# All additions of a Haar mixing phase on GpSimd, its transfers as single DMAs over 128 partitions, and the next phase's first work placed in the last rounds of the one before

## The chip, the cores and the metric

The kernel runs on one core of a Trainium2 chip. The metric is device time in microseconds (us), the median of several runs. Each profile is of one execution.

Short names used below: PE is TensorE, DVE is VectorE, ACT is ScalarE, POOL is GpSimd, SP is the engine that issues the DMAs.

## The reference

Four layers act in turn on x, a float32 array of shape (4, 64, 256, 256): a long convolution, a Haar layer with channel mixing, and two more long convolutions.

```python
def long_conv(x, ...):                      # layers 0, 2, 3
    k = outer product of two implicit filters per channel
    y = irfft2(rfft2(x, 512x512) * rfft2(k) / 512**2)[..., :256, :256]
    return y + x * bias[:, None, None]

def haar_layer(x, v, conv_w, tau):          # layer 1; v, tau (2,1,1,256,256), conv_w (2,64,64)
    f1 = haar2d(x)
    acc = 0
    for i in range(2):
        f4 = einsum('bchw,oc->bohw', f1 * v[i], conv_w[i])
        acc = acc + sign(f4) * relu(abs(f4) - tau[i])
    return haar2d(acc, inverse=True) + x
```

The kernel does each long convolution as two multiplications by Toeplitz matrices, one along each axis, because the filter is an outer product. Since the Haar transform is linear, `+ x` becomes an addition of the coefficients f1 to acc.

## The kernel before

There are three phases. **A** does layer 0 and the forward transform, channel pair by channel pair, and stores coefficients. **B** mixes the channels: a partition holds one channel of one half of the image rows, so 128 partitions are 64 channels by 2 halves. **C** does the inverse transform and layers 2 and 3. The four images are split into two groups. B's first half (group 0) runs beside A's second group, and B's second half (group 1) beside C's first group. "Beside" is literal: each phase is a list of small pieces, and the pieces of two lists are issued alternately.

```python
# phase A, one piece: rows, then columns, then products of the round before (each a third of a round)
def piece(t, j):
    now, last = t < total, t > 0
    ...
    if j < M:
        if now:  rows(t, j)                   # matmuls, eviction on ACT
        if last: run(st[t - 1]["ops"], 2)     # sums of the Haar transform, GpSimd
    elif j < 2 * M:
        if now:  columns(t, j - M)            # matmuls, then x1 = x*bias + psum on DVE (L302)
        ...
    else:
        if last: product(t - 1, j - 2 * M)    # matmuls with the Haar matrix
        if now:  run(st[t]["ops"], 2)
for t in range(total + 1):                    # the last turn has only products
    ...

# phase B, group grp; a unit u is one of the two mixings of a step of two image rows
def load(s):
    d["f"], d["v"], d["tau"] = ...            # 128-partition tiles, 4, 3 and 3 buffers
    for g in range(2):                        # two halves of 64 partitions
        part = slice(g * C, (g + 1) * C)
        nc.sync.dma_start(d["f"][part]..., coef[grp][:, rows]...)
        nc.sync.dma_start(d["v"][part]..., flat(v[rows]))
        nc.sync.dma_start(d["tau"][part]..., flat(taus[rows]))

def mix(u):                                   # PSUM pool of two buffers
    un[u]["f4"] = bps.tile([P, 2, W], F32, tag="f4", ...)
    for j in range(2):
        nc.tensor.matmul(un[u]["f4"][:, j, :], mix_sb[:, u % 2, :], f[:, j, :], ...)
def multiply(u):   nc.vector.tensor_tensor(f4, f4, v, ALU.mult)
def sign(u):       nc.scalar.activation(m, f4, AF.Sign)
def magnitude(u):  nc.scalar.activation(f4, f4, AF.Abs)
def less(u):       nc.vector.tensor_tensor(f4, f4, tau, ALU.subtract)
def threshold(u):
    o = un[u]["f4"] if u % 4 == 3 else un[u]["m"]
    nc.vector.scalar_tensor_tensor(o, un[u]["f4"], 0.0, un[u]["m"], ALU.max, ALU.mult)
def add(s, which):
    if which == 0:  nc.gpsimd.tensor_tensor(m0, m0, data(st[s]["f"]), ALU.add)
    elif s % 2:     nc.vector.tensor_tensor(g, m0, un[2 * s + 1]["f4"], ALU.add)   # L438
    else:           nc.gpsimd.tensor_tensor(g, m0, un[2 * s + 1]["m"], ALU.add)

def piece(u, j):
    s, i = divmod(u, 2)
    if j == 0:    mix(u); less(u - 1)
    elif j == 1:
        multiply(u); sign(u)
        threshold(u - 1); add((u - 1) // 2, 1 - i)
        if i == 0 and s >= 2:
            store(s - 2); load(s + 2)         # the store too: two halves of 64 partitions
    else:         magnitude(u)
...
# phase C, at its first piece
if t == 0:
    load(0); load(1); sums(0); run(st[0]["ops"], 16); filters(0)
...
beside(a[cut_a:], phase_b(0), 5 * M, M)
beside(c[:cut_c], phase_b(1), 2 * M, 10 * M)
beside(c[cut_c:], [], 0, 0)
```

In these traces each engine runs its instructions in the order in which the kernel issues them; a timeline further down shows VectorE idle for 1.14 us before A's L302, with B's multiply behind it in the order of issue, although the matmul that the multiply needs had ended. Two things follow. The next mix needs one of the two PSUM buffers, so it waits for the threshold (or, every fourth time, the addition) of the unit before last. And A's column addition L302 is on DVE in the same order as B's multiply.

## Time and profile before

| | before |
|---|---|
| device time | 3161.6 us (3160.7 to 3162.8, 3 runs) |
| PE busy | 2973.0 us of a span of 3159.3 us (94%) |
| A with B (first to last mix of B's first half) | 774 us, 6.10 us a mix, PE idle 94 us |
| handover (last mix to the first mix of B's second half) | 55 us, PE idle 31 us |
| C with B (B's second half) | 940 us, PE idle 13 us |
| DMA share in A with B | 1.03 at 269 GB/s |

The unit of 6.10 us is 774.1 us over the 127 distances between 128 mixes. The DMA share is the packets' time, summed, over the time of 16 engines; at 1, packets of all 16 DMA engines are in flight all the time, and it goes a little over 1 where packets overlap.

To read the page: the rows of 40 digits are slices of 79 us, a 9 being busy nine tenths or more. In a row of the costliest groups the numbers are the total busy time and the mean of one instruction, then the idle time of that engine just before those instructions, and what ended most of it. The POOL row of the page of the kernel before, and its row for the mixing matmul:

```profile
POOL 2776675666766766655556555565664444444441
...
L409 PE MATMUL f<-ft,mix_sb 128*128 128x512 f32 x1024 | 506.1, 617 | 112.6 <-DVE gt L438 57.3
```

GpSimd has room everywhere (no slice reaches 80%), and the mixing matmul is the only one of PE's with a large idle time before it. Its own mean of 617 ns will matter too.

### The profile page before, as it was taken

How to read it: one execution, taken by the hardware profiler on the slowest of the kernel's cores; microseconds unless marked ns; L12 is line 12 of the kernel's file. 1: busy time of each engine (PE TensorE's matmuls, PEld its weight loads, DVE VectorE, ACT ScalarE, POOL GpSimd, SP SyncE). 2: the span in 40 equal slices, each digit the busy share in tenths (PEclk: the TensorE clock that was granted, in tenths of full speed). 3: DMA queues.
4: the chain of work that ended last, by engine and by line, in shares of the span. 5: the costliest groups of instructions: out<-in, count | busy, mean ns of one | idle time of the engine just before them, and what ended most of it. 6: DMA issues, size and time to landing. Idle time of an engine off the chain costs nothing. (4 is left out here: it accounts for less than half of the span.)

```text
span 3159.3 us, 48195 instructions
## 1 busy us (share of the span) xinstructions
PE 2973.0 (94%) x17432; PEld 2535.1 (80%) x17432; DVE 1564.9 (50%) x1657; ACT 1230.2 (39%) x1799; POOL 1817.4 (58%) x2437
## 2 busy tenths in 40 slices
PE   5999999888988888599999999999999999999999
PEld 5989997666666666488877878887899999999998
DVE  2232213777777777457666667666732222222222
ACT  1333333444544445344444444444432222232222
POOL 2776675666766766655556555565664444444441
PEclk9999999999999999899999999999999999999999
DMA  6857898999999999789888988989744444444442
GB/s 159 215 179 193 226 234 226 258 274 272 274 275 270 274 277 265 230 195 268 233 244 226 250 231 238 249 226 255 205 141 132 141 124 124 124 138 132 127 120 87
DMA packets 380227, 656.76 MB, mean 208 GB/s; under 512 B 42134, under 2 KB 281399, under 8 KB 379992
## 3 DMA queue, kind: packets, MB, share of 16 engines
q1 hardware_dynamic: 379992, 653.69, 76.6%
q8 instruction: 140, 2.29, 0.3%
q14 instruction: 95, 0.78, 0.1%
HBM read 438.10 MB, written 215.42 MB: 207 GB/s over the span
## 5 line engine op out<-in xcount | busy, mean ns | idle before, releaser
L409 PE MATMUL f<-ft,mix_sb 128*128 128x512 f32 x1024 | 506.1, 617 | 112.6 <-DVE gt L438 57.3
L434 POOL TENSOR_TENSOR m<-m,ft 128x1024 f32<-128x1024 f32 x128 | 301.7, 2357 | 453.1 <-DVE m L429 441.4
L417 ACT ACTIVATE m<-f 128x1024 f32<-128x1024 f32 x256 | 262.5, 1025 | 513.1 <-DVE f L413 504.3
L546 DVE SCALAR_TENSOR_TENSOR cy<-cz,bias_sb,c1c 128x512 f32<-128x512 f32 x256 | 189.2, 746 | 515.9 <-PE c1c L224 515.9
L424 DVE TENSOR_TENSOR f<-f,tau 128x1024 f32<-128x1024 f32 x256 | 314.6, 1229 | 197.0 <-ACT f L420 194.2
L302 DVE SCALAR_TENSOR_TENSOR x<-x,bias_sb,a2ps 128x512 f32<-128x512 f32 x256 | 189.0, 745 | 428.8 <-PE a2ps L224 380.4
L409 PEld LDWEIGHTS f<-ft,mix_sb 128*128 128x128 f32 x1024 | 177.5, 193 | 258.3 <-issue 142.6
L546 DVE SCALAR_TENSOR_TENSOR o<-cy,bias_sb,c2c 128x512 f32<-128x512 f32 x256 | 189.5, 746 | 348.7 <-PE c2c L224 348.7
L413 DVE TENSOR_TENSOR f<-f,v 128x1024 f32<-128x1024 f32 x256 | 313.8, 1226 | 54.9 <-PE f L409 51.8
L223 PE MATMUL a1ps<-toep,x 128*128 128x256 f32 x1024 | 310.1, 385 | 21.3 <-DMA toep<-filt 18.1
L223 PE MATMUL a2ps<-toep,ay 128*128 128x256 f32 x1024 | 305.9, 381 | 1.8 <-ACT ay L292 1.8
L223 PE MATMUL c2r<-toep,cy 128*128 128x256 f32 x1024 | 305.8, 380 | 0.3 <-DVE cy L546 0.3
L223 PE MATMUL c1c<-toep,ch 128*128 128x256 f32 x1024 | 305.8, 380 | 0.0
L223 PE MATMUL c1r<-toep,cz 128*128 128x256 f32 x1024 | 305.8, 380 | 0.0
L223 PE MATMUL c2c<-toep,ch 128*128 128x256 f32 x1024 | 305.8, 380 | 0.0
L533 ACT COPY ch<-c2r 128x512 f32<-128x512 f32 x256 | 149.4, 588 | 382.4 <-PE c2r L224 382.2
L325 ACT ACTIVATE f<-a3ps,wcol_sb 128x512 f32<-128x512 f32 x256 | 175.7, 686 | 293.2 <-PE a3ps L317 251.5
L317 PEld LDWEIGHTS a3ps<-haarH_sb,fw 128*128 128x128 f32 x2048 | 244.9, 195 | 32.5 <-issue 22.7
L526 ACT COPY cz<-c1ps 128x512 f32<-128x512 f32 x256 | 148.1, 588 | 309.5 <-PE c1ps L522 309.5
L522 PEld LDWEIGHTS c1ps<-haarW_sb,ci 128*128 128x128 f32 x2048 | 238.8, 193 | 36.6 <-POOL ci L266 24.4
L522 PE MATMUL c1ps<-haarW_sb,ci 128*128 128x128 f32 x2048 | 244.6, 276 | 23.4 <-POOL ci L266 23.3
L420 ACT ACTIVATE f<-f 128x1024 f32<-128x1024 f32 x256 | 263.9, 1031 | 0.0
(64 smaller groups left out, 5868.5 us busy)
## 6 DMA issues: line engine op xcount, KB each, us to landing
toep<-filt SPq DMA_DIRECT2D x768, 128.0 KB, 4.1
x<-in_x SPq DMA_DIRECT2D x256, 256.0 KB, 7.8
coef<-f SPq DMA_DIRECT2D x128, 512.0 KB, 7.3
ft<-coef SPq DMA_DIRECT2D x256, 256.0 KB, 6.6
v<-in_v SPq DMA_DIRECT2D x256, 256.0 KB, 7.0
tau<-taus SPq DMA_DIRECT2D x256, 256.0 KB, 7.0
mixed<-gt SPq DMA_DIRECT2D x256, 256.0 KB, 6.0
g<-mixed SPq DMA_DIRECT2D x128, 512.0 KB, 5.4
```

The lines of the kernel that those rows point to most:

```text
L223: nc.tensor.matmul(ps[:, m, :], data[:, 0, cut], t[:, which, :], start=True, stop=False)
L302: nc.vector.scalar_tensor_tensor(s["x1"][:, cut], s["x"][:, cut], bias_sb[:, c : c + 1], ps, ALU.mult, ALU.add)
L317: nc.tensor.matmul(ps[:, e, bass.ts(k, P)], s["fw"][:, 2 * (n + e) + k, bass.ts(m, P)], haarH_sb[:, k, :], start=True, stop=True,)
L325: nc.scalar.activation(f4[:, n : n + 2, m, :], ps, AF.Copy, scale=wcol_sb[:, m : m + 1])
L409: nc.tensor.matmul(un[u]["f4"][:, j, :], mix_sb[:, u % 2, :], f[:, j, :], start=True, stop=True)
L413: nc.vector.tensor_tensor(f4, f4, weights(st[u // 2]["v"], u % 2), ALU.mult)
L417: nc.scalar.activation(un[u]["m"], un[u]["f4"], AF.Sign)
L420: nc.scalar.activation(un[u]["f4"], un[u]["f4"], AF.Abs)
L424: nc.vector.tensor_tensor(f4, f4, weights(st[u // 2]["tau"], u % 2), ALU.subtract)
L434: nc.gpsimd.tensor_tensor(m0, m0, data(st[s]["f"]), ALU.add)
L522: nc.tensor.matmul(ps[:, m, bass.ts(h, P)], s["ci"][:, 2 * n + h, bass.ts(m, P)], haarW_sb, start=True, stop=True)
L546: nc.vector.scalar_tensor_tensor(o, s["y", n], bias_sb[:, at : at + 1], ps, ALU.mult, ALU.add)
```

## The change

Three independent parts, which I name by a letter.

- **G**: every second step's addition moves from VectorE to GpSimd, which then does all of them. The point is to free the PSUM buffer one VectorE instruction earlier.
- **D**: partitions of B change their order from (half, channel) to (channel, half), so that each load and store of B is a single DMA over 128 partitions instead of two over 64.
- **P**: A's last turn (only products) is taken out of its list and put between C's first pieces. C's first loads and sums are issued in A's last two rounds, and B's first half is packed in front of those rounds.

The diff, cut to its core:

```diff
 # G
         def threshold(u):
-            o = un[u]["f4"] if u % 4 == 3 else un[u]["m"]
-            nc.vector.scalar_tensor_tensor(o, un[u]["f4"], 0.0, un[u]["m"], ALU.max, ALU.mult)
+            nc.vector.scalar_tensor_tensor(un[u]["m"], un[u]["f4"], 0.0, un[u]["m"], ALU.max, ALU.mult)
 ...
-                if s % 2:
-                    nc.vector.tensor_tensor(data(st[s]["g"]), m0, un[2 * s + 1]["f4"], ALU.add)
-                else:
-                    nc.gpsimd.tensor_tensor(data(st[s]["g"]), m0, un[2 * s + 1]["m"], ALU.add)
+                nc.gpsimd.tensor_tensor(data(st[s]["g"]), m0, un[2 * s + 1]["m"], ALU.add)
 # D   (mix_sb is built on the host in the new order; the first store's sums use a column of signs)
-            for g in range(2):
-                part = slice(g * C, (g + 1) * C)
-                rows = slice(g * C + r0, g * C + r0 + ROWS)
-                nc.sync.dma_start(d["f"][part]..., coef[grp][:, rows]...)
-                nc.sync.dma_start(d["v"][part]..., flat(v[rows]))
-                nc.sync.dma_start(d["tau"][part]..., flat(taus[rows]))
+            nc.sync.dma_start(d["f"].rearrange("p r b w -> p (r b w)"), rows_of(coef[grp], r0))
+            for name, src in (("v", v), ("tau", taus)):
+                flat = bass.AP(src.tensor, src.offset + r0 * 2 * W, [[0, C], [C * 2 * W, 2], [1, ROWS * 2 * W]])
+                nc.sync.dma_start(d[name].rearrange("p r i w -> p (r i w)"), flat)
+        def rows_of(ap, r0):
+            return ap.rearrange("c (g r) b h k -> c g r (b h k)", g=2)[:, :, r0 : r0 + ROWS].rearrange(
+                "c g r e -> c g (r e)")
 ...
-            for g in range(2):      # store, two halves
-                ...
+            nc.sync.dma_start(rows_of(mixed[grp], r0), gt.rearrange("p r b w -> p (r b w)"))
 # P
-        for t in range(total + 1):
+        for t in range(total):
 ...
+        last = [lambda: (coarsest(t - 1), store(t - 1), run(st[t]["ops"], 16))]
+        last += [lambda j=j: product(t, j) for j in range(M)]
+        last.append(lambda: (coarsest(t), store(t)))
 ...
-    beside(a[cut_a:], phase_b(0), 5 * M, M)
-    beside(c[:cut_c], phase_b(1), 2 * M, 10 * M)
+    beside(a[cut_a : -6 * M], phase_b(0), 5 * M, 0)
+    beside(a[-6 * M : -2 * M], c_first[:1], 2 * M, M)
+    beside(a[-2 * M :], c_first[1:], 0, 0)
+    main = a_last[:1] + c[:M]
+    for pair in zip(c[M : 2 * M], a_last[1:]):
+        main += pair
+    main += a_last[M + 1 :] + c[2 * M : cut_c]
+    beside(main, phase_b(1), 5 * M, 10 * M)
```

## The prediction

> **What bounds the kernel now.** I read the page first, for who is busy and when.
>
> ```profile
> PE 2973.0 (94%) x17432; PEld 2535.1 (80%) x17432; DVE 1564.9 (50%) x1657; ACT 1230.2 (39%) x1799; POOL 1817.4 (58%) x2437
> ...
> PE   5999999888988888599999999999999999999999
> ...
> PEclk9999999999999999899999999999999999999999
> DMA  6857898999999999789888988989744444444442
> ```
>
> TensorE is the bound, and idles 186 us of 3159.3. The idle is not spread out: the PE row drops to 8 in slices 8 to 16 (phase B's first half beside A) and to 5 in slice 17 (A hands over to C). The view by stretches cuts it there:
>
> ```profile
> 530.00:1304.00 774.00, 680.35 (x3397) 509.70 (x3396) 567.01 (x533) 377.12 (x494) 512.33 (x657) 0.98 1.03 269
> 1304.00:1343.00 39.00, 7.98 (x45) 6.75 (x43) 7.17 (x6) 6.95 (x10) 23.72 (x41) 0.65 0.66 204
> 1343.00:2282.00 939.00, 926.08 (x5087) 754.53 (x5088) 633.22 (x633) 418.40 (x592) 541.09 (x556) 1.00 0.88 237
> ```
>
> (Length, busy us of PE, PEld, DVE, ACT, POOL, then clock, DMA share, GB/s.) PE idles 94 us in A with B, 31 us in the handover, 13 us in C with B. After 2282 it is full and can't change. The first 40 us hold about 32 us of start-up idle, which the change hardly touches. The waits of PE in the first two stretches:
>
> ```profile
> PE f L409 <- DVE gt L438: 47.7, 30, 3.5
> PE f L409 <- DVE m L429: 37.4, 38, 2.7
> PE f L409 <- DMA ft<-coef: 11.4, 4, 7.2
> ```
>
> ```profile
> PE c1ps L522 <- POOL ci L266: 22.0, 1, 22.0
> PE a3ps L317 <- POOL fw L235: 9.0, 1, 9.0
> ```
>
> So in A with B the mixing matmul waits for a PSUM buffer (two of them) that VectorE frees; 47.7 us of it is for the addition on VectorE that the change removes. In the handover PE waits for GpSimd, which builds C's first sums only after A has ended.
>
> DMA is the hidden second bound. In A with B its share is 1.03. A stretch with nothing but B's loads (1346 to 1362) against one led by C's loads over 128 partitions (1324 to 1331):
>
> ```profile
> DMA packets 1060, 3.48 MB, mean 217 GB/s; under 512 B 214, under 2 KB 214, under 8 KB 1059
> ```
>
> ```profile
> DMA packets 628, 2.29 MB, mean 327 GB/s; under 512 B 71, under 2 KB 71, under 8 KB 627
> ```
>
> B's halves over 64 partitions run at 217 GB/s with the engines full, the others at 327. In the packet records a 4 KB packet takes 320 ns (median) in the first stretch and 159 ns in the second.
>
> **What the Trainium skill says.** (1) "SBUF — State Buffer", Door 1: partitions 0 to 63 reach 8 of 16 ports, asymptote about 218 GB/s, and only one transfer that spans 128 partitions reaches all. The 217 above agree. (2) "GPSIMD Engine Reference", 3.1: a two-input addition costs about twice what it does on VectorE (4497 against 2293 ns at 2048 elements). Here 2357 ns (L440) against 1221 ns (L438) at 1024: agrees. (3) "SBUF — State Buffer", Who interferes with whom: a VectorE instruction with one SBUF input does not contend with GpSimd. B's VectorE work has one input in PSUM, so more additions on GpSimd should not slow it; no run yet shows it.
>
> **The change part by part.**
>
> *Additions.* 64 additions leave VectorE and 64 go to GpSimd, half of them in each half of B. Between mixes of one 2-unit step VectorE has five or six 1024-element instructions (about 1.13 us start to start). The gt wait falls on every fourth mix: 30 waits, 1.6 us each. The other mixes wait 37.4/95 = 0.4 us on average. If the fourth ones become like them, 32 x (1.5 - 0.4) = 35 us go, 0.27 us a unit. GpSimd's cost: 10.4 us a round for A's sums (16 rows summed) and 0.6 for the coarsest pair, plus now one 2.32 us addition a unit instead of three in four: at 4.6 units a round 21.8 us of about 25.5, 85%. Near, not over; A's sums have four pieces (5 us) of slack before their product.
>
> *Packing.* B's first half was spread over 373 pieces of A and is now spread over 340, so that A's last two rounds run without it. 394 B pieces over 340 are 1.16 a piece against 1.06; A pieces between two mixes fall from 2.84 to 2.59. An A piece is 14 us / 12 = 1.17 us of PE (from timelines: 4 x 1.31 rows, 4 x 1.31 columns, 4 x 0.88 products) and a mix 1.82. PE's own work a unit falls from 5.14 to 4.84 us; the measured unit is 774/127 = 6.09. But not all of this 0.29 is won. In the loop mix, multiply, threshold of the unit before, mix, VectorE runs in order: with a column addition (L302, waiting for its own matmuls 1.31 us) ahead of the multiply the loop lasts 1.98 + 1.31 + 0.7 + 1.2 + 1.2 = 6.4 us, whatever PE has to do. In the product third it lasts about 5.1 (ScalarE's two passes and evictions); in the rows third PE itself bounds, about 5.2. By thirds of a round of 4.64 units: 1.55 x (6.15 + 5.1 + 5.2) = 25.4 us, or 5.5 a unit, plus 0.1 of throttled clock: **5.6 us a unit** against 6.09. 127 x 5.6 = 711 us, 63 fewer. Against that A now still has 34 pieces (40 us) after B's last mix, where before it had 17 us including 9 of wait: 24 lost. Net 39.
>
> *Handover.* Those two rounds hide B's last store, C's load and the 11.9 us of sums on GpSimd. Before, PE waited 22 us, and ran A's last products and C's first at 0.6 of the clock (5.4 us each instead of 3.7), 3 us. I expect about 4 us of wait for the first sums (they can start only once A's penultimate sums are off GpSimd) and 6 us for the last A product, whose sums (10.4 us) come behind C's on GpSimd while PE has only 5 us of C to do; 3.5 us of A's products also move behind it. Net 22 + 3 - 4 - 6 - 3.5 - 1 of clock, about 10.
>
> *Transfers.* Bytes are the same, DMAs fall by half (512 fewer). If a packet takes 159 instead of 320 ns, DMA stops being full in A with B. PE waits little for it now, so directly this is worth only a few us (4). But without it the rate could hardly rise: DMA is already full at 6.09 us a unit.
>
> *C with B.* The gt waits there are 9.6 us; 8 go. B's second half starts only 7 pieces after A's last store instead of well after it: 4 us back.
>
> *Start.* 4 fewer small loads and a memset: 1.
>
> Sum: 39 + 10 + 4 + 8 - 4 + 1 = 58; I shade it to 53 for work the loop will find to wait for. 3161.6 - 53 = **3108 us** (1.7%).
>
> **The rivals.** *DMA stays full.* The source of the new transfers has two outer steps (64 channels by 2 halves), and if the 16 engines then take neighbouring eights of partitions, two still meet on one port, and packets stay at 320 ns. With B at 4.2 us of DMA a unit and A at 1.58 the unit can't fall below 5.8: A with B gives 25 us less, total about 3133. For it: today's saturation. Against: the toeplitz loads, with an outer 16 by 8, mostly take 46 ns a KB, undisturbed. One in four. *The loop is freer than I think.* If the fast DMA and the missing addition leave PE the bound (4.84 + 0.2), 127 x 0.55 = 70 us more: 3038. Against: L302's place in VectorE's order is untouched. A mild form (5.3 a unit) gives 3070. *GpSimd becomes the bound.* At 85% and in order, an addition that waits for VectorE holds A's sums, and the product waits for fw: each us a round costs 27 us. For it: the 9 us wait on fw at the end of A. Against: four pieces of slack, and PE never waits on fw elsewhere. With 1 us a round: 3135. *It is only moved*: if the loop holds 6.09, packing A's rounds behind B adds 24 us and the rest wins 19, so 3166; against it, 47.7 us of waits that name a removed instruction.
>
> **Range and chances.** Main uncertainty: the unit in A with B, 5.35 to 5.85 (32 us either way), then the handover (10 us). Range 3070 to 3138. Two per cent is 3098.4, 10 us under my point: faster 0.36, same 0.61, slower 0.03.
>
> **What would show it.** A with B: mixes 5.6 us apart; waits on gt gone from PE, waits on m L429 about as large as both together (60 to 85 us). Handover: PE idle 8 to 14 us instead of 31, on ci and fw. DMA share in A with B under 0.9 at 280 GB/s or more, 4 KB packets mostly near 159 ns; if 320, the first rival. GpSimd 66% busy overall (1817 + 64 x 2.33 = 1966 us), its L440 rows at 2357 ns x128, VectorE's rows unchanged. PE waits on fw inside A would show the third rival. The prediction fails upward if the loop frees itself, downward if DMA or GpSimd takes the place of VectorE.

## More of the kernel before

Each kernel was run beside the kernel before, on the same chip in the same batch, and its ratio is taken there. Where two changed kernels of different batches are compared, the difference is that of their medians; the kernel before had medians of 3160.1 to 3162.9 us over the batches, so such differences are good to 2 or 3 us.

## The result, and the profile after

| | before | after |
|---|---|---|
| device time, median | 3162.2 us (3160.7 to 3164.3, 4 runs) | 3088.6 us (3086.5 to 3093.4, 4 runs) |
| PE busy / span of the profiled run | 2973.0 / 3159.3 us | 2958.1 / 3085.9 us |
| A with B | 774 us, 6.10 a mix, PE idle 94 | 698 us, 5.50 a mix, PE idle 68 |
| handover | 55 us, PE idle 31 | 76 us, PE idle 8 |
| C with B | 940 us, PE idle 13 | 925 us, PE idle 9 |
| DMA share in A with B | 1.03 at 269 GB/s | 0.87 at 294 GB/s |
| 4 KB packet there, median | 259 ns | 159 ns |

The ratio of after to before is 0.9769, with a 95% interval of 0.9752 to 0.9786: **2.3% faster**. The result is correct. The handover now holds two rounds of A that the first stretch held before, so the stretches must be read together.

The page of the changed kernel:

```profile
PE 2958.1 (96%) x17432; PEld 2529.5 (82%) x17432; DVE 1489.8 (48%) x1593; ACT 1233.1 (40%) x1799; POOL 1964.8 (64%) x2500
...
PE   6999999898989898899999999999999999999999
...
POOL 2776776787888888766666667667664444444441
...
DMA  6857997888989897576676776766544444444442
...
L409 PE MATMUL f<-ft,mix_sb 128*128 128x512 f32 x1024 | 495.3, 606 | 75.4 <-DVE m L427 72.1
L435 POOL TENSOR_TENSOR gt<-m,m 128x1024 f32<-128x1024 f32 x128 | 302.1, 2360 | 208.1 <-DVE m L427 147.5
```

The 5 in PE's row, the handover (slice 17), has become an 8; of the eight 8s in A with B (slices 8 to 16) five are left. VectorE has lost 64 instructions, GpSimd has gained them (L435 now 128 times, at the old duration) and still has slack. The mixing matmul waits 37 us less, and one takes 606 ns instead of 617.

The view by stretches of the changed kernel: A with B, the handover, C with B (columns as in the prediction):

```profile
525.10:1223.30 698.20, 629.92 (x3140) 468.99 (x3141) 521.40 (x490) 367.23 (x474) 560.35 (x642) 0.99 0.87 294
1223.30:1299.10 75.80, 67.78 (x439) 62.83 (x439) 17.73 (x21) 26.23 (x41) 64.48 (x112) 0.95 0.49 171
1299.10:2224.40 925.30, 916.71 (x5046) 746.15 (x5045) 606.90 (x610) 420.09 (x592) 608.88 (x573) 1.00 0.70 240
```

The waits of PE in A with B, and then in the handover (us in total, times, longest):

```profile
PE f L409 <- DVE m L427: 68.1, 67, 4.1
PE f L409 <- DMA ft<-coef: 3.1, 1, 3.1
```

```profile
PE c1ps L513 <- POOL ci L266: 5.7, 1, 5.7
PE a3ps L317 <- POOL fw L235: 2.4, 1, 2.4
```

The waits on the addition are gone; nearly all that is left is for the threshold, which is what the prediction named. In the handover two short waits replace 22 and 9 us. The instructive question is how much of the 74 us belongs to which part.

### The profile page after: what moved, and what is told of

Its sections match the earlier page's. It is cut to its first block, busy times and chain, and to the rows that moved or that the text cites. A ratio compares the mean times of both kernels' runs of the same rounds, so it can differ in the third digit from the quotient of the medians. Undisturbed runs are those within 1.5% of the kernel's fastest.

```text
span 3085.9 us, 47693 instructions
## 1 busy us (share of the span) xinstructions
PE 2958.1 (96%) x17432; PEld 2529.5 (82%) x17432; DVE 1489.8 (48%) x1593; ACT 1233.1 (40%) x1799; POOL 1964.8 (64%) x2500
## 4 chain that ended last, share of the span: by engine, by line
PE 78%; DVE 6%; POOL 3%; issue 2%; DMA 2%; ACT 1%; SPq 0%; DVEq 0%; POOLq 0%; ACTq 0%
PE f L409 12%; PE c1r L223 7%; PE c1ps L513 7%; PE c1c L223 7%; PE c2r L223 7%; PE c2c L223 7%; PE a1ps L223 5%; PE a2ps L223 4%; PE c1r L224 4%; PE c1c L224 4%; PE c2r L224 3%; PE c2c L224 3%; PE a3ps L317 3%; DVE m L427 2%; PE a1ps L224 2%
## 5 line engine op out<-in xcount | busy, mean ns | idle before, releaser
L409 PE MATMUL f<-ft,mix_sb 128*128 128x512 f32 x1024 | 495.3, 606 | 75.4 <-DVE m L427 72.1
L435 POOL TENSOR_TENSOR gt<-m,m 128x1024 f32<-128x1024 f32 x128 | 302.1, 2360 | 208.1 <-DVE m L427 147.5
L424 DVE TENSOR_TENSOR f<-f,tau 128x1024 f32<-128x1024 f32 x256 | 314.7, 1229 | 231.6 <-ACT f L420 231.6
L302 DVE SCALAR_TENSOR_TENSOR x<-x,bias_sb,a2ps 128x512 f32<-128x512 f32 x256 | 189.2, 745 | 430.7 <-PE a2ps L224 346.2
L413 DVE TENSOR_TENSOR f<-f,v 128x1024 f32<-128x1024 f32 x256 | 313.6, 1225 | 23.7 <-PE f L409 22.0
L427 DVE SCALAR_TENSOR_TENSOR m<-f,m 128x1024 f32<-128x1024 f32 x256 | 310.7, 1214 | 0.5 <-DVE f L424 0.5
L264 POOL TENSOR_TENSOR i<-g 128x8 f32<-128x8 f32 x64 | 14.2, 222 | 389.1 <-DMA g<-mixed 389.0
```

The lines of the kernel that those rows point to most:

```text
L413: nc.vector.tensor_tensor(f4, f4, weights(st[u // 2]["v"], u % 2), ALU.mult)
L424: nc.vector.tensor_tensor(f4, f4, weights(st[u // 2]["tau"], u % 2), ALU.subtract)
L427: nc.vector.scalar_tensor_tensor(un[u]["m"], un[u]["f4"], 0.0, un[u]["m"], ALU.max, ALU.mult)
L435: nc.gpsimd.tensor_tensor(data(st[s]["g"]), m0, un[2 * s + 1]["m"], ALU.add)
```

## The experiments

The theory was that the additions open the loop in A with B and that the single DMAs matter mainly because the DMA engines were about to become the bound. The rivals were that one part carries the gain alone, that the transfers do all of it, and that the remaining waits are not from the order of VectorE's instructions. All twelve kernels gave correct results.

### Each part alone

**Only the transfers.** The edit is part D of the diff and nothing else:

```diff
+            nc.sync.dma_start(d["f"].rearrange("p r b w -> p (r b w)"), rows_of(coef[grp], r0))
 # likewise v, tau and the store; threshold, add and the order of pieces as in the kernel before
```

> The kernel before with one part of the change alone: B's transfers as single DMAs over 128 partitions (with the layout and constants they need). Theory 1 (the handshake mix, multiply, threshold sets the pace in A with B; DMA is only just below it): 5 to 12 us faster, mixes about 6.0 us apart, the DMA share in A with B falls from 1.03 to about 0.85, PE's waits on VectorE stay near 85 us. Theory 2 (port sharing of the 64-partition DMAs was the real limit of A with B, although no compute engine is shown to wait for it): 35 us faster or more, mixes 5.75 us apart or less.

Measured: 3148.7 us, ratio 0.9955 (0.994 to 0.9969), 14 us less, a little over what theory 1 allowed. The DMA share in A with B fell to 0.80, and the median 4 KB packet to 159 ns, so the first rival of the prediction (packets stay slow) is out. PE's waits in A with B:

```profile
PE f L409 <- DVE gt L438: 52.4, 31, 3.5
PE f L409 <- DVE m L429: 37.3, 39, 2.4
PE f L409 <- DMA ft<-coef: 3.6, 1, 3.6
```

The wait on DMA goes from 11.4 to 3.6 us, the wait on VectorE stays (85.1 before, 89.7 now). With a fifth of the DMA capacity idle, VectorE holds the unit at 6.01 us.

**Only the additions.** Part G alone:

```diff
-                if s % 2:
-                    nc.vector.tensor_tensor(data(st[s]["g"]), m0, un[2 * s + 1]["f4"], ALU.add)
+                nc.gpsimd.tensor_tensor(data(st[s]["g"]), m0, un[2 * s + 1]["m"], ALU.add)
```

> The kernel before with one part alone: all additions of B on GpSimd. Theory 1: 20 to 35 us faster (30 waits of 1.6 us become waits of 0.4), mixes about 5.85 us apart, DMA share over 1.03 still. Theory 2: under 12 us faster, because DMA, already full, takes the place of the wait; PE or VectorE then show waits on ft, v or tau.

Measured: 3147.8 us, ratio 0.9948 (0.993 to 0.9965), 15 us less. C with B is 12.2 us shorter (927.6 instead of 939.8 us between its first and last mix), but A with B only 6.6 us (767.5 instead of 774.1), and the handover is 3.7 us longer. PE's waits in A with B:

```profile
PE f L410 <- DVE m L428: 49.3, 48, 3.4
PE f L410 <- DMA ft<-coef: 39.6, 19, 7.1
```

The addition's wait has gone, and a wait for B's loads has come in its place, 39.6 us where there were 11.4. The DMA share is 1.04. The unit is 6.04 us. The 15 us lie between the two ranges: the wait for loads that theory 2 named came, but did not take everything.

**Only the placement.** Part P alone:

```diff
-    beside(a[cut_a:], phase_b(0), 5 * M, M)
+    beside(a[cut_a : -6 * M], phase_b(0), 5 * M, 0)
+    ...
```

> The kernel before with one part alone: the placement (B's first half packed into 340 pieces, A's last two rounds and C's first loads and sums overlapped). Theory 1: 5 to 20 us faster: 25 to 30 us of handover idle go, 24 us of A's rounds come behind B, and packing wins about 0.1 to 0.15 us a unit of 127. Theory 2: mixes stay at 5.95 or more since DMA cannot go faster, so within 8 us of before.

Measured: 3163.2 us, ratio 1.0002 (0.9985 to 1.0019): nothing. PE's idle time in the handover fell from 31.0 to 10.7 us and that in A with B rose from 93.7 to 106.2 us, although that stretch then held two rounds of A less. Theory 2 gave the time and nearly the unit (5.93 us), but not the reason alone: with fast DMAs and the same placement (D and P, below) the unit is 5.92 us as well.

### Each part left out

The complements fill in the rest of the eight combinations. **Without the transfers** (G and P):

```diff
+            for g in range(2):        # the 64-partition halves of the kernel before, put back
+                part = slice(g * C, (g + 1) * C)
+                ...
-            nc.sync.dma_start(d["f"]..., rows_of(coef[grp], r0))
```

> The changed kernel without the single DMAs (B's transfers as 64-partition halves again, in the layout of before). Theory 1: DMA binds at about 5.8 us a unit, so 30 to 40 us slower than the changed kernel (3120 to 3130), with a DMA share over 1.03 in A with B. A theory in which the single DMAs matter only through fewer issues and lower latency: under 12 us slower, mixes at 5.6 or less.

Measured: 3150.8 us, ratio 0.996 (0.9946 to 0.9975). That is 62 us slower than the changed kernel, where theory 1 had said 30 to 40. PE waits 51.6 us for B's loads in A with B, at a DMA share of 1.04, and the unit is 5.92 us instead of the 5.8 expected.

**Without the additions** (D and P):

```diff
+                if s % 2:             # every second addition is on VectorE again
+                    nc.vector.tensor_tensor(data(st[s]["g"]), m0, un[2 * s + 1]["f4"], ALU.add)
```

> The changed kernel with a quarter of the additions back on VectorE as before. If the VectorE addition costs what its waits said (35 us over A with B, 8 in C with B): 35 to 45 us slower than the changed kernel, waits on gt of VectorE back at 40 to 55 us. If the packing and the fast DMA absorb it: under 20 us slower.

Measured: 3151.0 us, ratio 0.9958 (0.9942 to 0.9975), again 62 us slower than the changed kernel, where 35 to 45 were expected. PE's waits on the addition are back at 55.3 us in A with B, and the DMA share is 0.80.

**Without the placement** (D and G):

```diff
-    beside(a[cut_a : -6 * M], phase_b(0), 5 * M, 0)
-    ...
+    beside(a[cut_a:], phase_b(0), 5 * M, M)
+    beside(c[:cut_c], phase_b(1), 2 * M, 10 * M)
```

> The changed kernel with the placement of before. PE idle in the handover back at about 31 us. By my sum the placement is worth: handover 24 us, less 24 us of A behind B, plus packing 0.1 to 0.2 us a unit: 15 to 30 us slower than the changed kernel; mixes 5.6 to 5.7 us apart against 5.50.

Measured: 3089.7 us, ratio 0.9767 (0.9753 to 0.9782). That is the whole gain; the 15 to 30 us expected of the placement are not there (1 us). The stretches of this kernel, A with B and handover:

```profile
526.50:1242.10 715.60, 663.36 (x3396) 502.24 (x3396) 528.09 (x502) 377.83 (x493) 585.86 (x694) 0.99 0.85 291
1242.10:1300.70 58.60, 25.98 (x140) 23.83 (x141) 8.19 (x8) 12.06 (x18) 37.59 (x56) 0.68 0.67 232
```

The handover keeps its 33 us of idle PE (58.60 - 25.98) and its clock of 0.68, and yet B's second half starts at 1300.7 us, where the changed kernel starts it at 1299.1.

All eight together, as us against the kernel before (difference of the medians of the same batches), with the mix distance in A with B:

| parts | us | us a mix | DMA share |
|---|---|---|---|
| none | 0 | 6.10 | 1.03 |
| D | -14 | 6.01 | 0.80 |
| G | -15 | 6.04 | 1.04 |
| P | 0 | 5.93 | 1.04 |
| G and P | -12 | 5.92 | 1.04 |
| D and P | -12 | 5.92 | 0.80 |
| D and G | -73 | 5.63 | 0.85 |
| D, G and P | -74 | 5.50 | 0.87 |

With P the same 128 mixes share fewer pieces of A, so 5.93 and 5.50 compare with each other, and 6.10 and 5.63. D and G gain little alone and 73 us together: two floors of nearly the same height, DMA with 64-partition halves and VectorE with the addition, 6.04 and 6.01 us a unit without P, 5.92 and 5.92 with it. Taking away one exposes the other. G is worth 59 us on top of D (3148.7 to 3089.7). D is worth 62 us as the last of the three (3150.8 to 3088.6).

### What makes the single DMA better

D changes the number of DMAs, their span of partitions and the order of the partitions. Two kernels split them again into as many DMAs as before, both with the new order. **Two DMAs of 64 partitions each:**

```diff
-            nc.sync.dma_start(d["f"]..., rows_of(coef[grp], r0))
+            for h in range(2):
+                part, cs = slice(h * C, (h + 1) * C), slice(h * C // 2, (h + 1) * C // 2)
+                nc.sync.dma_start(d["f"][part]..., rows_of(coef[grp], r0)[cs])
 # likewise v, tau and the store
```

> The changed kernel with each of B's four transfers a step cut into two DMAs of 64 neighbouring partitions (channels 0 to 31, 32 to 63), packets of 4 KB as now. If the ports decide: 4 KB packets back at about 320 ns in A with B, DMA share over 1.0, as slow as the changed kernel without single DMAs (25 to 40 us slower than the changed kernel).

**Two DMAs of 128 partitions, half of each row:**

```diff
-            nc.sync.dma_start(d["f"]..., rows_of(coef[grp], r0))
+            e = ROWS * W
+            for h in range(2):
+                part = slice(h * e, (h + 1) * e)
+                nc.sync.dma_start(d["f"]...[:, part], rows_of(coef[grp], r0)[:, :, part])
 # likewise v, tau and the store
```

> The changed kernel with each of B's four transfers a step cut into two DMAs that both span 128 partitions (half of each row, packets of 2 KB). As many DMAs as before the change, but all ports. If the ports decide: within 6 us of the changed kernel, DMA share under 0.95 in A with B. If the number of DMAs decides (issue time on the queue's engine, completions): as slow as the one cut by partitions.

Measured: 3134.2 us (ratio 0.9907, 0.989 to 0.9923) for 64 partitions, and 3092.0 us (0.9773, 0.9758 to 0.9787) for 128. The first line is A with B of the kernel with 64, the second of that with 128:

```profile
527.20:1268.20 741.00, 642.20 (x3140) 475.17 (x3141) 523.00 (x490) 366.96 (x474) 560.16 (x640) 0.97 1.03 274
```

```profile
523.50:1226.00 702.50, 631.55 (x3140) 469.87 (x3141) 521.53 (x490) 367.56 (x474) 561.54 (x643) 0.99 0.90 293
```

With the same number of DMAs the span decides: share 1.03 at 274 GB/s against 0.90 at 293, and 38 us of stretch, although the kernel with full span has the smaller packets. With 64 partitions the median 4 KB packet in A with B took 247 ns (320 were expected, 259 is the kernel before) and the kernel was 46 us slower than the changed one (25 to 40 expected). Doubling the number at full span costs 3 us (3088.6 to 3092.0). This agrees with the Trainium skill, "SBUF — State Buffer", section "Can I just issue two DMAs to hit both halves?", which says that only one transfer that spans all 128 partitions reaches all ports (the prediction gives this sentence under Door 1; it stands here). What stays open: the kernel with two of 64 is still 17 us faster than the changed kernel without D (3134.2 against 3150.8), and no run tells whether the order of the partitions or the sources of v and tau cause that. In the traces the difference lies in the DMAs: 247 against 266 ns for the median 4 KB packet in A with B, 274 against 270 GB/s.

### What bounds the loop now

The prediction blamed L302, A's column addition, which stands ahead of the multiply in VectorE's order and waits for its own matmuls. The changed kernel shows such a turn (a view in order of time: start, duration, engine, line; what was waited for is in brackets):

```profile
998.70 1.88 PE L409 MATMUL f<-ft,mix_sb 128*128 128x512 f32 x4
...
1001.93 0.75 DVE L302 SCALAR_TENSOR_TENSOR x<-x,bias_sb,a2ps 128x512 f32<-128x512 f32 x1 [1.14 <-PE a2ps L224]
...
1002.59 1.23 DVE L413 TENSOR_TENSOR f<-f,v 128x1024 f32<-128x1024 f32 x1
1003.73 1.22 DVE L427 SCALAR_TENSOR_TENSOR m<-f,m 128x1024 f32<-128x1024 f32 x1
...
1005.00 1.55 PE L409 MATMUL f<-ft,mix_sb 128*128 128x512 f32 x3 [1.80 <-DVE m L427]
```

The mix is done at 1000.6, its product could be multiplied then, but VectorE waits for PE's column matmuls, does L302, and only then multiplies and thresholds. The next mix waits 1.80 us for that threshold and starts at 1005.0, 6.3 us after this one (the view ends before its fourth matmul). The experiment issues the multiply, the sign and the threshold in the same piece as the mix, so that no piece of A comes between:

```diff
             if j == 0:
                 if u < units:
                     mix(u)
                 if 0 < u <= units:
                     less(u - 1)
-            elif j == 1:
                 if u < units:
                     multiply(u)
                     sign(u)
 ...
-            elif u < units:
+            elif j == 1 and u < units:
                 magnitude(u)
```

> The changed kernel with the multiply, the sign pass, the threshold of the unit before and its addition emitted in the same piece as the mixing matmul, so that no column addition (L302) of A stands on VectorE between the mix and the multiply; the magnitude pass one piece later. If L302's place makes the 6.4 us loop in the column third: waits of PE on VectorE in A with B fall from 68 to about 35 to 45 us, mixes about 5.3 us apart, 20 to 35 us faster than the changed kernel. If GpSimd or DMA is the next bound at once: under 8 us faster, with waits of PE on ft or fw instead.

Measured: 3030.0 us, ratio to before 0.9574 (0.9558 to 0.959), so 58.5 us under the changed kernel. PE's idle time in A with B fell from 68 to 20 us and the unit from 5.50 to 5.05 us. PE's waits there:

```profile
PE f L409 <- DVE m L427: 19.6, 28, 3.4
PE f L409 <- DMA ft<-coef: 4.0, 1, 4.0
```

The edit moves more than the multiply: B's addition, store and load are also issued one piece earlier, and the sign pass stands earlier on ScalarE. PE's waits on loads were 3.1 us before it and 4.0 after, so the loads are not what it won. And the traces show where it won. Take the distances between mixes in which at least four fifths of A's matmul time is of one kind. In the column third, where L302 stands, the unit falls from 6.01 to 5.00 us and PE's idle time from 21.5 to 0 us; in the rows third the unit falls from 5.32 to 5.25, in the product third from 4.67 to 4.44. The cause is confirmed; my expectation of its size (20 to 35 us) was too small.

**The magnitude as well**, in the same piece:

```diff
                     sign(u)
+                    magnitude(u)
 ...
-            elif j == 1 and u < units:
-                magnitude(u)
```

> As the last, with the magnitude pass emitted right behind the sign pass too, so that ScalarE's evictions of A do not stand between them. If the second loop (multiply, sign, magnitude, tau subtraction, next multiply) limits the product third: another 10 to 20 us, mixes about 5.1 us apart, 3045 to 3060 us in all. If evictions of A that now come later starve PE: slower than the last one, with waits of PE on ay or on a3 banks.

Measured: **3026.1 us** (3025.0 to 3026.9), ratio 0.9562 (0.9548 to 0.9576), only 4 us better than the last one, where I had expected 10 to 20. The reason given for it did not hold either: the product third stays at 4.43 us a unit (4.44 with the last kernel), and it is the rows third that falls, from 5.25 to 5.07. So the second loop in the product third is not what was left. It is the fastest kernel here: 4.4% under the kernel before, 2.0% under the changed one. The same place in its trace:

```profile
1001.73 1.98 PE L409 MATMUL f<-ft,mix_sb 128*128 128x512 f32 x4
...
1003.74 1.23 DVE L413 TENSOR_TENSOR f<-f,v 128x1024 f32<-128x1024 f32 x1
...
1004.88 1.21 DVE L427 SCALAR_TENSOR_TENSOR m<-f,m 128x1024 f32<-128x1024 f32 x1
...
1006.01 1.40 DVE L302 SCALAR_TENSOR_TENSOR x<-x,bias_sb,a2ps 128x512 f32<-128x512 f32 x2
...
1007.47 1.88 PE L409 MATMUL f<-ft,mix_sb 128*128 128x512 f32 x4
```

The multiply starts as the mix ends, L302 comes behind the threshold, and the next mix has no wait in brackets. PE is busy 617.8 of 633.9 us in this stretch, at a DMA share of 0.96 and 324 GB/s. GpSimd, the third rival, is at 558.5 of 633.9 us (88%) there and still not waited for. The next floor is near by this estimate: a share of 0.96 in a unit of 4.99 us is 4.8 us of DMA a unit.

**With the loop open, is the placement worth something?** The same edit on the kernel without P:

```diff
 # the kernel without the placement, with the same edit of B's piece
                     sign(u)
+                    magnitude(u)
 ...
```

> The last kernel with the placement of before. With the loop open, PE should bound A with B, so that A's two rounds behind B are no longer paid twice: the placement is then worth its handover idle, 20 to 27 us, where between the changed kernel and the one without placement it was worth 1. If the loop still binds, under 8 us.

Measured: 3032.5 us, ratio 0.9584 (0.9569 to 0.9599), so the placement is worth 6.4 us there, where I had expected 20 to 27. That is in the range that I had set for a loop that still binds, but the loop doesn't: PE is idle for only 5.9 us of A with B in this kernel. PE's whole idle time (span less busy) is 88.0 us without it and 76.5 us with it; but the same 17432 matmuls are busy 2942.5 us without and 2948.6 us with it. So it wins 11.5 us of idle and loses 6.1 us in longer matmuls. The other pairs show the same two signs: to the kernel before, to D alone, to G alone and to D with G, P removes 5.3, 8.8, 3.9 and 6.0 us of idle and adds 5.5, 14.9, 6.4 and 2.7 us of busy time. The clock records of the traces explain some of this: matmuls that ran at half the clock (see the section on the prediction) cost 15.4 us more with P next to D, 5.6 next to G and 2.5 next to the kernel before, but 1.2 less next to D with G, and only 0.4 more here. So it is the clock in the pairs with D alone and with G alone; in the last two it is not, and why the matmuls lengthen there stays open.

**With the loop open, are the transfers worth more?** The same edit on the kernel without D:

```diff
 # the kernel without the single DMAs, with the same edit of B's piece
                     sign(u)
+                    magnitude(u)
 ...
```

> The fastest kernel so far (early multiply, sign and magnitude) with B's transfers as 64-partition halves again. If DMA is a floor of its own in A with B at about 5.9 us a unit: mixes 5.85 to 5.95 us apart, 3140 to 3150 us in all, PE's waits on ft over 80 us and on VectorE under 20, so that the single DMAs are worth 115 us or more here, against 14 alone. If the floor is the loop's latency with DMA only adding to it: 3060 to 3100.

Measured: 3150.3 us, ratio 0.9969 (0.9952 to 0.9986; the kernel before took 3160.1 us on that chip). Opening the loop gives nothing at all there (3150.8 without it). A with B, and PE's waits in it:

```profile
530.60:1283.00 752.40, 662.41 (x3140) 485.64 (x3141) 524.77 (x491) 366.84 (x474) 562.13 (x639) 0.93 1.04 271
```

```profile
PE f L410 <- DMA ft<-coef: 72.9, 25, 7.3
PE f L410 <- DVE m L428: 12.6, 17, 3.6
```

The wait on VectorE is all but gone and B's loads have taken its place, at 5.92 us a unit, as with G and P (5.92). So DMA with those halves is a floor of 5.92 us a unit in its own right, and with the loop open D is worth 124 us (3150.3 to 3026.1).

## Why the prediction was right or wrong

The range held (3070 to 3138), the point of 3108 was 19 us too slow, and the class that I gave 0.61, within 2%, was not the one that came: the 2% line lay 10 us under the point and the result 10 us beyond it. The mechanism was right in its main step; the sizes were off in both directions. That the point came so near is in part luck: the placement gave 9 us less than its term, and that cancelled part of the 25 us that the other two parts gave over theirs. Taking the parts in the order D, then G, then P (the order matters: they don't add), the medians give 14, 59 and 1 us:

| term, as predicted | us predicted | us measured |
|---|---|---|
| transfers 4 and start 1 | 5 | 14 (before to D alone) |
| additions, 35 in A with B and 8 in C with B | 43 | 59 (D alone to D with G) |
| placement: packing 28 (63 less 35), A's rounds behind B -24, handover 10, B's late start -4 | 10 | 1 (D with G to all) |
| sum | 58, shaded to 53 | 74 |

**The additions: right in idle time, wrong in leaving PE's own time constant.** From D alone to D with G the same 3396 matmuls of A with B take 47.3 us less. PE's idle time there falls by 37.7 us, where I had worked out 35, and in C with B by 8.4 us, where I had 8. The rest, 9.6 and 4.0 us, is busy time. A with B of D alone (its counterpart with G is above), and the mixing matmul there, first D alone, then D with G:

```profile
526.40:1289.30 762.90, 672.98 (x3396) 506.13 (x3396) 565.98 (x533) 376.83 (x493) 515.35 (x664) 0.99 0.80 273
```

```profile
L409 PE MATMUL f<-ft,mix_sb 128*128 128x512 f32 x508 | 256.1, 628 | 93.5 <-DVE gt L438 52.4 <-DVE m L429 37.3 <-DMA ft<-coef 3.6
L409 PE MATMUL f<-ft,mix_sb 128*128 128x512 f32 x508 | 249.8, 614 | 56.3 <-DVE m L427 51.8 <-DMA ft<-coef 4.1
```

The sum treated idle time as the only cost of a wait. The Trainium skill, "TensorE: Matmul & The Clock Gate", Part 1, says that idle windows of PE lower its clock. The clock records in the traces (times and granted share; no view prints them one by one) agree, and give the size. The granted clock is 1.00 or 0.50. In A with B it is 0.50 for 22.9 us in six stretches with D alone, and for 8.4 us in two with D and G. A mixing matmul takes 610 ns on average outside such stretches and 1070 inside (D alone). Against the median of the same matmul at full clock, those that touch a half-clock stretch cost 13.6 us more with D alone and 5.0 with D and G: 8.6 of the 9.6 us. A's matmuls that fall into such a stretch lengthen too. The 4.0 us in C with B are something else, since the clock is 1.00 there in both kernels; they stay open. The prediction had put 0.1 us a unit (13 us) of lowered clock into the new loop and had counted none for the old one; in A with B the half clock cost 21.7 us before and 6.9 after.

**The transfers: the enabling right, the direct effect too small.** "Without it the rate could hardly rise" is what the kernel without D shows, with PE waiting 51.6 us on loads. The direct gain was put at 4 us: PE's idle time in A with B did fall by 3.7 us (93.7 to 90.0), but its busy time fell too, by 7.4 us (680.4 to 673.0), and the first mix came 3.1 us earlier (529.5 to 526.4), where I had 1 us of start. The missing term is the same as above: the half clock cost 21.7 us there before and 13.6 with D alone. The first rival's floor of 5.8 us a unit was close to the 5.92 measured; its trigger, slow packets with two outer steps in the source, did not come.

**The placement: the step that failed.** I let the packing pay 63 less 35, or 28 us, of which 24 were given back, and then counted 10 us of handover on top. Measured, from D with G to all parts: the stretch to the last mix shortens by only 17.4 us (715.6 to 698.2) and the handover lengthens by 17.2 us (58.6 to 75.8), so B's second half starts 1.6 us earlier. Of the 24.6 us of idle that left the handover (32.6 to 8.0), 16.0 reappeared in A with B (52.3 to 68.3) and 3.6 in C with B (5.0 to 8.6). Packing more mixes into fewer pieces of A takes away the PE work that had hidden VectorE's loop. I knew the loop (6.4 us in the column third, 6.3 seen), and still let most of the packing through. The rival named "it is only moved" described this part well, though not the whole. Sorted by thirds of A as above, the changed kernel's unit is 6.0 us in the columns, 5.3 in the rows and 4.7 in the products, where the sum took 6.15, 5.2 and 5.1: the loop itself was read nearly right, and what failed was the share of the gain that was put down to the packing.

**The other marks.** Waits on the threshold were to be 60 to 85 us: 68. The handover waits were to be 4 us on the first sums and 6 on the last product: 5.7 and 2.4. GpSimd was to be 66% busy (a slip: its own 1966 us are 63% of 3108): 64%, and inside A with B PE never waited on A's sums. The DMA share was to be under 0.9 at 280 GB/s or more: 0.87 at 294. B's second half was to lose 4 us at its start: no such wait shows; PE's idle time there is 8.6 us in all. The mix distance was to be 5.6 us: 5.50. Two small slips in the working changed nothing that matters: it takes 6.15 us for the column third just after deriving 6.4, and at the start two small loads go, not four (the four of mix_sb become one, and one for the column of signs is new).

**The loop.** That L302's place in VectorE's order was the next bound is shown by the 58.5 us that moving B's work ahead of it gave, most plainly in the column third. The mild form of the second rival (5.3 us a unit) did not come with this change; the loop had to be opened by hand.

## What to carry to other kernels

When one resource is at a share of 1 and another holds the main engine by waits, measure each fix alone and with the other: here they gave 14 and 15 us alone and 73 together, and the waits of the kernel before named only one of the two. Where an engine serves two phases in the order of issue, issue a short dependent chain (matmul, multiply, threshold) in one piece, before the other phase's instructions that wait for their own matmuls (58.5 us here). Idle time that a new placement removes in one stretch has to be followed into the stretch that lost the work.

## What the runs showed of the hardware that I had not expected

- The same 17432 matmuls took between 2942.5 and 2993.0 us of PE's busy time. Nearly all of the difference is the clock: matmuls at half clock cost 10.7 us in the first kernel (loop open, no placement) and 57.2 us in the second (loop open, halves of 64). The half-clock time grows with PE's idle time, but not by its sum alone: in A with B, 90.0 us of idle came with 22.9 us of it in D alone, where the longest wait was 3.6 us, and with 100.8 us in the second of these kernels, where waits on loads were up to 7.3 us. The mixing matmul, which does nearly all the waiting, ranged in its mean from 599 ns (loop open, no placement) to 636 ns (loop open, halves of 64); the 256-wide Toeplitz matmuls of C stayed at 380 to 382 ns. Of the 73.6 us gained, about 15 are PE's busy time (2973.0 to 2958.1), and 13 of these are the clock (26.2 to 13.3 us).
- A DMA share of 1.03 showed only 11.4 us of PE's waits on DMA, because VectorE's loop happened to be as long. A share of 1.04 showed 39.6, 51.6 and 72.9 us once VectorE was faster.
- Twice as many DMAs of half the size, over 128 partitions, cost only 3 us of 3089.

## What the Trainium skill lacked or had wrong

- "Perfetto Trace Analysis", Identifying the Most-Contended Engine, tells to optimize the most contended engine first. It lacks the case of two floors of nearly the same height, where the waits name only one: fixing either gave 14 or 15 us of 3162, both gave 73.
- "TensorE: Matmul & The Clock Gate", A second HAM failure mode, says that frequent short idle times of PE lower its throughput, but not how much half-clock time waits of a given length and number bring: here 90.0 us of idle in A with B, in waits of at most 3.6 us, came with 22.9 us of it, and 52.3 us, in waits of at most 4.1 us, with 8.4.
- "SBUF — State Buffer", Door 1, gives all 16 ports to a transfer over partitions 0 to 127. It doesn't say whether one whose source has outer steps of 64 by 2 still reaches them all, nor does "DMA: Bandwidth & Descriptors", whose table of engines and ports for a 128-partition transfer leaves the shape of the source unsaid. Here nothing was lost: 4 KB packets took 159 ns (median) instead of 259, as they did in the transfers without such a source.
- Nothing was found wrong: the addition on GpSimd stayed at 2360 ns (2357 before) beside VectorE's work, and VectorE's multiply and subtraction of tau at 1225 and 1229 ns (1226 and 1229), as "SBUF — State Buffer", Who interferes with whom, has it.
